# A selective-scan block on one core: nesting over halves of the channels and pairs of states, with b from row-tiled 64-token diagonal blocks

## Chip, cores and metric

The kernel runs on one core of one Trainium2 chip. The metric is the device time of an execution in microseconds (us). One execution of each kernel is also taken by the hardware profiler; its span is given beside the times.

## What is computed

x has 8 rows of 2048 tokens with 512 channels, in fp32. The reference is a layer norm, a selective scan (S6) with a residual, a second layer norm and an int8 matmul with a residual:

```python
xp = jnp.einsum('bld,ed->ble', x, x_proj_w)          # 64 of dt, 16 of B, 16 of C
delta = jax.nn.softplus(jnp.einsum('blr,dr->bld', d_rank, dt_proj_w) + dt_proj_b)
deltaA = jnp.exp(jnp.einsum('bld,dn->bldn', delta, A))
deltaB_u = jnp.einsum('bld,bln,bld->bldn', delta, Bm, x)
    h = dA_t * h + dBu_t
    y = jnp.einsum('bdn,bn->bd', h, C_t)
y = ys.transpose(1, 0, 2) + x * D
...
x = x + _L0_attn_ref(_layernorm(x, axis=-1), ...)
x = x + _L0_ffn_ref(_layernorm(x, axis=-1), ...)     # rows scaled by max|x|/127, rounded, times int8 weights
```

For each of 512 channels and 16 states there is one recurrence over the tokens of a row: h = da * h + b, with da = exp(delta * A) and b = delta * x * B. The output of a channel is the sum of h * C over its states.

## The kernel before

**Tiling.** The tokens are cut into 32 chunks of T = 512, four to a batch row. In a chunk there are 16 states n and 4 tiles d of 128 channels: 64 units of (state, channel tile), and to each unit belongs a *slot* of the order in which instructions are issued. Channels lie on the 128 partitions and tokens along the free axis.

**One unit.** ACT computes da, one exp of 128x512 (exp_unit, L742). PE writes b into one PSUM bank (b_pe, L777 to L796), and DVE runs the scan over 512 tokens (L804), reading da from SBUF and b from PSUM. The b of a unit is made in one of two ways. For the six states of DIAG_STATES, delta * x (tokens on partitions, 128 tokens in each of four blocks) is multiplied by a diagonal matrix with B on its diagonal (L786); these diagonal blocks dg are kept in DRAM, zeroed once, their diagonals are stored for each chunk (store_diagonals, L262) and a state's blocks of 256 KB are loaded in bt_piece (L759). For the other ten states, ACT scales delta * x by B, token by token (bT, L772), and PE transposes it (L795).

**Four units, one state.** POOL starts the group with a carry (L756): it puts the state at the end of the last chunk, times the first da, into the first column. It ends with one product h * c over 128x2048 (c_mult, L830), where c is a row of C loaded from DRAM to all partitions (load_c, L814). ACT keeps the last column (keep_state, L839). PE turns the products back to tokens on partitions and sums them over the states in PSUM (y_pe and y_halves, L860), eleven slots behind the scans, in two row halves of 64. The skip D * x (L881) and the residual x (add_x, L585) are added in the same banks.

**Around the units.** While chunk k is scanned, steps of chunk k+1 (prep) and of chunk k-1 (post) stand in given slots of PREP_AT and POST_AT (LATE_AT for the last two). In prep: norm (L287), transposes (L299), projection (L311), the transposes to BT and their copy (slot 26, L331 and L340), the projection to delta (dt_pe, L350), its softplus on ACT (slots 27, 31, 32 and 34, L360), transposes of delta (dlt_pe, slots 35 to 41, L368) and their product with x (du, L373). In post: the residual copies on ACT (L612), statistics on DVE (L242, L246), nmr on POOL (L252 to L258), the norm z on ACT (slots 29, 29, 32 and 34, L618), the largest absolute value on DVE (amax, slots 33 and 35, L637), scaling, rounding, int8 matmul and output (o_out, L686).

**What sets the order.** Every engine runs its instructions in the order in which the program issues them (pin). In a slot come the state copy and the carry, the product, the load of c, the exps, bT, b two slots ahead, the scan, y and then the planned steps. EXP_NONE names 22 slots without an exp, 28 to 34 among them, and EXP_TWO 22 slots with two:

```python
        want += 0 if slot in EXP_NONE else 2 if slot in EXP_TWO else 1
        while want and slot not in EXP_NONE and ahead < (s + 3) * ND:
            exp_unit(ahead)
```

**Buffers.** da, h and hc have three each (of 4 units), c five, dg two, bT three. PSUM: y in two tiles of two banks, b in three banks, one bank (ps_m) for everything else.

## Time and profile before

| | us |
|---|---|
| median of three runs | 2850.26 |
| lowest and highest | 2842.12, 2853.73 |
| span of the profiled execution | 2848.6 |
| busy in it: POOL | 2771.5 |
| PE | 2739.1 |
| DVE | 2731.4 |
| ACT | 2723.7 |

The profiled execution's own time is not given apart from its span; the median lies 1.7 us above the span. 2048 scans take 2363.2 us of DVE (1201 ns each, starts 1.11 us apart where they follow one another), 511 products 2328.1 us of POOL, 2048 exps 1381.8 us and 1276 pieces of bT 896.5 us of ACT. How to read the views: a busy time overlaps with that of other engines; the waits name the engine whose result came last; a timeline gives start, length, engine, line, operation and count of instructions that follow each other.

### The profile page before, as it was taken

The page shows a single profiled execution, that of the slowest core. Times are in us where ns is not written, and L with a number is a line of the kernel's source. Part 1 is how long each engine was busy: PE and PEld are TensorE (multiplying, and loading weights), DVE is VectorE, ACT ScalarE, POOL GpSimd, SP SyncE. Part 2 cuts the span into 40 slices and gives each one's busy share as a digit, 9 for nine tenths or more (in the row PEclk, how much of TensorE's full clock was granted, in tenths as well). Part 3 has the DMA queues.
Part 4 walks back from the last instruction along what each step waited for, and adds up shares of the span by engine and source line. Part 5 has one row for each costly group of instructions (what it writes and reads, how often), then busy time and mean ns, then how long its engine had stood idle before and what let it go on. Part 6 is the DMA issues. An engine that isn't in the chain of part 4 may idle for free.

```text
span 2848.6 us, 80379 instructions
## 1 busy us (share of the span) xinstructions
PE 2739.1 (96%) x33032; PEld 2357.2 (83%) x33032; DVE 2731.4 (96%) x2949; ACT 2723.7 (96%) x4762; POOL 2771.5 (97%) x1243
## 2 busy tenths in 40 slices
PE   8999999999999999999999999999999999999988
PEld 6888888888888888888888888888888878888877
DVE  6999999999999999999999999999999999999998
ACT  7999999999999999999999999999999999999995
POOL 6899999999999999999999999999999999999998
PEclk9999999999999999999999999999999999999999
DMA  5333343434434334444344343344444443434332
GB/s 151 107 92 95 106 113 109 109 80 105 113 109 116 87 97 110 106 117 105 85 106 111 109 118 85 101 109 106 116 104 89 106 109 109 111 81 102 100 99 71
DMA packets 260528, 295.90 MB, mean 104 GB/s; under 512 B 118144, under 2 KB 118656, under 8 KB 260160
## 3 DMA queue, kind: packets, MB, share of 16 engines
q1 hardware_dynamic: 259104, 290.53, 39.7%
q8 instruction: 259, 4.24, 0.6%
q14 instruction: 109, 0.89, 0.1%
q10 hardware_dynamic: 1056, 0.23, 0.0%
HBM read 252.55 MB, written 38.14 MB: 102 GB/s over the span
## 4 chain that ended last, share of the span: by engine, by line
PE 68%; DMA 9%; DVE 9%; ACT 5%; issue 4%; POOL 3%; SPq 1%; DVEq 0%; POOLq 0%; ACTq 0%
PE pb L786 22%; PE y L860 14%; PE pb L795 13%; DMA dg<-dg 8%; DVE h L804 7%; PE y L585 3%; PE po L677 3%; PE y L881 3%; PE pxp L311 2%; ACT da L742 2%; PE pdl L368 2%; POOL hc L830 2%; PE pz L660 2%; PE pxn L299 2%; ACT bT L772 2%
## 5 line engine op out<-in xcount | busy, mean ns | idle before, releaser
L804 DVE TENSOR_TENSOR_SCAN h<-da,pb 128x512 f32<-128x512 f32 x2048 | 2363.2, 1201 | 91.7 <-PE pb L786 51.7
L830 POOL TENSOR_TENSOR hc<-h,c 128x2048 f32<-128x2048 f32 x511 | 2328.1, 4563 | 20.2 <-DVE h L804 6.8
L742 ACT ACTIVATE da<-delta,a_neg 128x511 f32<-128x511 f32 (+1 forms) x2048 | 1381.8, 716 | 1.0 <-DVE h L804 0.6
L772 ACT ACTIVATE bT<-x,BT 128x512 f32<-128x512 f32 x1276 | 896.5, 715 | 0.0
L786 PE MATMUL pb<-dg,x 128*128 128x128 f32 x6176 | 785.6, 279 | 45.4 <-DMA dg<-dg 39.4
L786 PEld LDWEIGHTS pb<-dg,x 128*128 128x128 f32 x6176 | 739.2, 192 | 86.4 <-DVE h L804 45.5
L795 PE MATMUL pb<-ident,bT 128*128 128x128 f32 x5104 | 720.2, 276 | 23.6 <-DVE h L804 10.9
L795 PEld LDWEIGHTS pb<-ident,bT 128*128 128x128 f32 x5104 | 581.7, 141 | 183.8 <-issue 70.9
L860 PE MATMUL y<-ident,hc 64*128 64x64 f32 x16384 | 613.6, 226 | 1.9 <-DVE hc L899 1.0
L860 PEld LDWEIGHTS y<-ident,hc 64*128 64x128 f32 x16384 | 547.7, 139 | 75.4 <-issue 49.5
L242 DVE BATCH_NORM_STATS2 st<-x 128x6 f32<-128x512 f32 x244 | 156.3, 671 | 0.0
L350 PE MATMUL pdt<-xp,dtproj_sb 128*128 128x512 f32 x248 | 138.5, 640 | 11.9 <-ACT delta L360 11.4
L698 POOL TENSOR_TENSOR z<-z,x 128x1024 f32<-128x1024 f32 x62 | 147.6, 2380 | 0.0
L630 POOL TENSOR_TENSOR x<-x,bias_b 128x1024 f32<-128x1024 f32 x62 | 146.7, 2367 | 0.1
L881 PE MATMUL y<-diag_d,xnT 64*128 64x64 f32 x2048 | 138.7, 275 | 0.0
L881 PEld LDWEIGHTS y<-diag_d,xnT 64*128 64x128 f32 x2048 | 124.8, 188 | 10.7 <-issue 10.7
L677 PE MATMUL po<-wq_sb,qT 128*128 128x512 bf16 x496 | 127.6, 380 | 0.0
L360 ACT ACTIVATE delta<-pdt,dtb_sb 128x512 f32<-128x512 f32 x124 | 84.9, 685 | 44.6 <-PE pdt L350 43.7
L585 PE MATMUL y<-x,ident 128*128 128x256 f32 x512 | 127.4, 381 | 0.0
L311 PE MATMUL pxp<-xnT,xproj_sb 128*96 128x512 f32 x248 | 123.1, 598 | 0.0
L618 ACT ACTIVATE z<-x,nmr,rstd 128x512 f32<-128x512 f32 x124 | 97.1, 807 | 9.5 <-POOL nmr L258 9.5
L585 PEld LDWEIGHTS y<-x,ident 128*128 128x128 f32 x512 | 90.5, 192 | 8.6
(112 smaller groups left out, 1716.9 us busy)
## 6 DMA issues: line engine op xcount, KB each, us to landing
c<-bc SPq DMA_DIRECT2D x512, 256.0 KB, 3.5
dg<-dg SPq DMA_DIRECT2D x191, 256.0 KB, 4.7
x<-in_x_dram SPq DMA_DIRECT2D x64, 512.0 KB, 4.8
x<-in_x_dram SPq DMA_DIRECT2D x31, 1024.0 KB, 6.7
out_dram<-z SPq DMA_DIRECT2D x62, 512.0 KB, 4.6
dg<-zeros SPq DMA_DIRECT2D x12, 256.0 KB, 5.3
dg<-BT SPq DMA_DIRECT2D x192, 2.0 KB, 6.7
x<-in_x_dram SPq DMA_DIRECT2D x4, 256.0 KB, 4.4
```

Of the source, the lines that this page charges most:

```text
L242: pin(nc.vector.bn_stats(st, src))
L311: nc.tensor.matmul(st["pp"][:E], lhsT=xproj_sb[:, d, :], rhs=xn_t[k][:, d, :], start=(d == 0), stop=(d == ND - 1),)
L585: nc.tensor.matmul(ys[k, i // 2][:, half, i % 2, :, :], lhsT=ident, rhs=t[:, :, half, :], start=False, stop=False, skip_group_check=True,)
L677: nc.tensor.matmul(po, lhsT=qt[:, d, :], rhs=wq_sb[:, d, :], start=(d == 0), stop=(d == ND - 1))
L742: nc.scalar.activation(das[s][:, d, own], delta[k][:, d, own], AF.Exp, scale=a_neg[:, d, n : n + 1])
L772: nc.scalar.activation(bts[s][:, i, :], xn[k][:, i, :], AF.Copy, scale=b_t[k][:, i, n : n + 1])
L786: nc.tensor.matmul(pb[:, ts(i, P)], lhsT=xn[k][:, i, ts(d, P)], rhs=bts[s][:, i, :], start=True, stop=True,)
L795: pin(nc.tensor.transpose(pb[:, ts(i, P)], bts[s][:, i, ts(d, P)], ident))
L804: nc.vector.tensor_tensor_scan(hs[s][:, d, :], das[s][:, d, :], pbs.pop(u), 0.0 if k % CPB == 0 else 1.0, ALU.mult, ALU.add,)
L830: pin(nc.gpsimd.tensor_tensor(hc, h, c.unsqueeze(1).to_broadcast([P, ND, T]), ALU.mult))
L860: nc.tensor.matmul(ys[k, i // 2][:, half, i % 2, d, :], lhsT=hc[rows, d, ts(i, P)], rhs=ident[rows, rows], is_transpose=True, start=first, ...
L881: nc.tensor.matmul(ys[k, i // 2][:, half, i % 2, d, :], lhsT=xn_t[k][rows, d, ts(i, P)], rhs=diag_d[rows, d, rows], start=False, stop=Fals ...
```

## The change

The units of a chunk are nested anew: first over the two halves dp of the channels (two tiles each), in each over eight pairs of states, the second half backwards from the last pair. A group is still four units: two tiles by two states, and still has one product on POOL, one carry and one state copy.

The b of both states of a pair is made for one channel tile at once, for all states from diagonal blocks. A block now has 64 tokens: its rows are half of the partitions, its 128 columns are 64 tokens by two states. Eight matmuls, two row halves for each of four blocks, fill a tile of two banks (two such tiles), and the scans read it with a stride of two elements. bT and its ACT instructions are gone. Diagonals are stored by two transfers of 8-byte elements a chunk (six of 4-byte elements before); the blocks of a pair are loaded by 256 KB and its two rows of c by 512 KB, and the last three pairs of the first half are used again at the start of the second. Three blocks are made by POOL at the start; eight zeroing stores go to each DRAM buffer, six before.

So that a block of 64 tokens lies in one bank, tokens are interleaved over the partitions: partition p holds tokens 4p to 4p + 3 in x, and transposes, projections and copies in prep write or read with a stride of four. y has one tile of two banks, used twice a chunk; the residual of the first half is copied in slots 44 and 45, that of the second in 12 and 13 of the next chunk. ps_m has two banks. The add_x matmuls are one for each half. EXP_NONE and EXP_TWO are gone: one exp is issued in every slot, seven ahead. Steps of prep and post keep their slots.

The core of the diff (left out: the start's transposes and projections in the new order of tokens, the tail's copies, and changes of names and shapes alone):

```diff
-DIAG_STATES = [1, 3, 5, 9, 10, 13]
...
-LAST_LOAD = (30, 56)
-LAST_ADD_X = (50, 52, 61, 62)
-SKIP_AT = (43, 46, 55, 60)
-EXP_NONE = (2, 4, 6, 8, 9, 11, 14, 16, 20, 28, 29, 30, 31, 32, 33, 34, 46, 48, 49, 50, 54, 56)
-EXP_TWO = (0, 1, 3, 5, 7, 17, 18, 22, 23, 25, 35, 38, 41, 47, 51, 53, 55, 57, 59, 61, 62, 63)
+MADE_HERE = 3
+REUSED = 3
+LOAD_AT = (18, 20)
+SKIP_AT = (16, 18, 20, 22)
+ADD_X_AT = (24, 26)
+FIRST_HALF_AT = (44, 45)
...
+    dgp = ctx.enter_context(tc.tile_pool(name="dgp", bufs=5))
...
-    ps_b = ctx.enter_context(tc.tile_pool(name="ps_b", bufs=3, space=bass.MemoryType.PSUM))
-    ps_m = ctx.enter_context(tc.tile_pool(name="ps_m", bufs=1, space=bass.MemoryType.PSUM))
+    ps_b = ctx.enter_context(tc.tile_pool(name="ps_b", bufs=2, space=bass.MemoryType.PSUM))
+    ps_m = ctx.enter_context(tc.tile_pool(name="ps_m", bufs=2, space=bass.MemoryType.PSUM))
...
-        pin(nc.sync.dma_start(out=t, in_=xf[k]))
+        pin(nc.sync.dma_start(out=t, in_=xq[k]))
         xn[k] = t
+
+    def turned_tokens(t, i):
+        return t.rearrange("p (q i) -> p i q", i=NT)[:, i]
...
+    dg_dram = [diagd.tile([P, NPAIR, NT, HALF, 2], F32, name=f"dg_{j}") for j in range(2)]
...
     def store_diagonals(k):
         dg = dg_dram[k % 2]
-        for j, n in enumerate(DIAG):
+        row = NPAIR * NT * HALF * 2
+        for h in range(2):
             pin(
                 nc.sync.dma_start(
                     out=bass.AP(
                         tensor=dg.tensor,
-                        offset=dg.offset + j * P * NT * P,
-                        ap=[[NT * P + 1, P], [P, NT]],
+                        offset=dg.offset + h * HALF * row,
+                        ap=[[row + 2, HALF], [HALF * 2, NPAIR * NT], [1, 2]],
                     ),
-                    in_=b_t[k][:, :, n],
+                    in_=b_t[k][ds(h * HALF, HALF)].rearrange("p g i n -> p (g i) n"),
...
+    def turn_tokens(out, src, i, n):
+        pin(
+            nc.tensor.matmul(
+                out,
+                lhsT=turned_tokens(src, i),
+                rhs=ident[:n, :n],
+                is_transpose=True,
+                start=True,
+                stop=True,
+            )
+        )
...
-                pin(nc.tensor.transpose(pt[:, ts(i, P)], xn[k][:, i, ts(d, P)], ident))
+                pin(nc.tensor.transpose(turned_tokens(pt, i), xn[k][:, i, ts(d, P)], ident))
...
-                pin(nc.tensor.transpose(pt[:, ts(d, P)], delta[k][:, d, ts(i, P)], ident))
+                turn_tokens(pt[:, ts(d, P)], delta[k][:, d, :], i, P)
...
+        for s in range(MADE_HERE):
+            dgs[0, s] = dgp.tile([P, NT, HALF, 2], F32, tag="dg", name=f"dg_0_{s}")
+            pin(
+                nc.gpsimd.tensor_tensor(
+                    dgs[0, s],
+                    mask.unsqueeze(1).unsqueeze(3).to_broadcast([P, NT, HALF, 2]),
+                    bt[:, s].unsqueeze(2).to_broadcast([P, NT, HALF, 2]),
+                    ALU.mult,
+                )
+            )
...
+    def add_x(k, dp, half):
+
+        t = x1[k].rearrange("p i (d h c) -> p i d h c", h=2, c=HALF)[:, :, ds(2 * dp, 2), half, :]
+        pin(
+            nc.tensor.matmul(
+                ys[k, dp][:, half, :, :, :],
+                lhsT=ident,
+                rhs=t,
+                start=False,
+                stop=False,
+                skip_group_check=True,
+            )
+        )
...
+    def load_x1(k, j):
+        if j == 0:
+            x1[k] = work.tile([P, NT, DM], F32, tag="x1", bufs=2, name=f"x1_{k}")
+        two = ds(2 * j, 2)
+        pin(nc.sync.dma_start(out=x1[k][:, two, :], in_=xf[k][:, two, :]))
+
+    def residual(k, dp, half):
+        t = x1[k].rearrange("p i (d h c) -> p i d h c", h=2, c=HALF)[:, :, ds(2 * dp, 2), half, :]
+        pin(nc.scalar.copy(t, ys[k, dp][:, half, :, :, :]))
...
+    def place(s):
+        k, g = divmod(s, GROUPS)
+        dp, at = divmod(g, NPAIR)
+        return k, dp, at if dp % 2 == 0 else NPAIR - 1 - at
...
+    def of_unit(u):
+        s, j = divmod(u, 4)
+        k, dp, np_ = place(s)
+        return s, k, 2 * dp + j // 2, 2 * np_ + j % 2, j % 2, j // 2
...
-                das[s][:, d, own], delta[k][:, d, own], AF.Exp, scale=a_neg[:, d, n : n + 1]
+                das[s][:, n2, d2, own], delta[k][:, d, own], AF.Exp, scale=a_neg[:, d, n : n + 1]
...
+    def reused(s):
+        return (s % GROUPS) // NPAIR % 2 == 1 and s % NPAIR < REUSED
...
+        t = dgp.tile([P, NT, HALF, 2], F32, tag="dg", name=f"dg_{s}")
+        pin(nc.sync.dma_start(out=t, in_=dg_dram[k % 2][:, np_]))
+        dgs[k, np_] = t
+
+    def b_pe(v):
...
+        pb = ps_b.tile([P, 2, HALF, NT, 2], F32, tag="b", name=f"pb_{s}_{d2}")
         for i in range(NT):
-            if is_diag(k, n):
+            for h in range(2):
+                rows = ds(h * HALF, HALF)
                 pin(
                     nc.tensor.matmul(
-                        pb[:, ts(i, P)],
-                        lhsT=xn[k][:, i, ts(d, P)],
-                        rhs=bts[s][:, i, :],
+                        pb[:, h, :, i, :],
+                        lhsT=xn[k][rows, i, ts(d, P)],
+                        rhs=dgs[k, np_][rows, i, :, :],
...
+                hs[s][:, n2, d2, :],
+                das[s][:, n2, d2, :],
+                pbs[u // 2].rearrange("p h q i n -> p (h q i) n")[:, :, n2],
...
+        if s >= LAST or reused(s):
             return
-        k, n = divmod(s, N)
-        t = bcp.tile([P, T], F32, tag="c", name=f"c_{k}_{n}")
-        pin(nc.sync.dma_start(out=t, in_=bcs[k][n, :].partition_broadcast(P)))
-        cts[s] = t
+        k, dp, np_ = place(s)
+        t = bcp.tile([P, 2, T], F32, tag="c", name=f"c_{s}")
+        pin(nc.sync.dma_start(out=t, in_=bcs[k][ds(2 * np_, 2), :].partition_broadcast(P)))
+        cts[k, np_] = t
...
+        hc = work.tile([P, 2, 2, T], F32, tag="hc", bufs=3, name=f"hc_{s}")
+        c = cts[k, np_]
+        pin(
+            nc.gpsimd.tensor_tensor(
+                hc, h, c.unsqueeze(2).to_broadcast([P, 2, 2, T]), ALU.mult
+            )
+        )
...
+                    ys[k, dp][:, half, i, d2, :],
+                    lhsT=hc[rows, ts(i, P)],
...
-        plan(k * SLOTS, [(SKIP_AT[i], lambda k=k, i=i: skip_pe(k, i)) for i in range(NT)])
+        plan(k * SLOTS, [(LOAD_AT[j], lambda k=k, j=j: load_x1(k, j)) for j in range(2)])
+        for dp in range(DP):
+            at = (k * DP + dp) * SLOTS // DP
+            plan(
+                at,
+                [(SKIP_AT[i], lambda k=k, dp=dp, i=i: skip_pe(k, dp, i)) for i in range(NT)]
+                + [(ADD_X_AT[h], lambda k=k, dp=dp, h=h: add_x(k, dp, h)) for h in range(2)],
+            )
+        plan(
+            k * SLOTS,
+            [(FIRST_HALF_AT[h], lambda k=k, h=h: residual(k, 0, h)) for h in range(2)],
+        )
...
-            load_c(s + 3)
-
-        want += 0 if slot in EXP_NONE else 2 if slot in EXP_TWO else 1
-        while want and slot not in EXP_NONE and ahead < (s + 3) * ND:
+            load_c(s + 2)
+            load_dg(s + 2)
+        if ahead < (s + 3) * 4:
             exp_unit(ahead)
             ahead += 1
-            want -= 1
         if k < NCHUNK:
-            bt_piece(s + 2, d)
-            b_pe(u + 2)
+            if u % 2 == 0:
+                b_pe(u // 2 + 1)
```

## The prediction

> **What bounds the kernel now.** I read the page's busy times first, then a table of stretches, then the waits of the two busiest engines, then timelines of one chunk.

> ```profile
> PE 2739.1 (96%) x33032; PEld 2357.2 (83%) x33032; DVE 2731.4 (96%) x2949; ACT 2723.7 (96%) x4762; POOL 2771.5 (97%) x1243
> ```

> Four engines over 95% say little: a PE matmul counts as busy until its modelled end, and any of the four could lead. The stretch from 208 to 2736 us, 28.9 chunks of 87.35 us, repeats itself (columns: PE, PEld, DVE, ACT, POOL):

> ```profile
> 208.00:2736.00 2528.00, 2454.16 (x29747) 2111.66 (x29745) 2455.69 (x2628) 2462.24 (x4310) 2497.74 (x1099) 1.00 0.41 104
> ```

> Per chunk that is 86.3 us of work for POOL, 84.85 for DVE, 85.1 for ACT. Their waits in that stretch, largest first:

> ```profile
> POOL ve L252 <- DVE mv L246: 9.4, 20, 0.7
> ```

> ```profile
> DVE h L804 <- PE pb L786: 36.0, 80, 2.0
> DVE h L804 <- PE pb L795: 20.7, 62, 0.6
> ```

> POOL waits 17.8 us in all 28.9 chunks, DVE 64.3 (2.2 a chunk). So POOL is the bound and DVE follows 1.5 us a chunk behind; neither has room. POOL's own list (products 4563 ns each, 16 a chunk, carries, two kinds of additions) is left by the change as it is. It can therefore gain at most the 17.8 us; it can lose as much as DVE is held up beyond POOL's lead.

> **Where the change bites: the order on ACT.** Before, no exp stands in slots 28 to 34, where the four softplus stand. The table is switched twice a chunk:

> ```profile
> L742 ACT ACT_TABLE_LOAD x32 | 41.1, 1283 | 0.6
> L360 ACT ACT_TABLE_LOAD x31 | 39.8, 1283 | 0.6
> ```

> One chunk of it (start, length, what):

> ```profile
> 1463.16 0.20 ACT L340 COPY BT<-pbt 128x64 f32<-128x64 f32 x1
> ...
> 1464.62 1.28 ACT L360 ACT_TABLE_LOAD   x1
> ...
> 1466.59 1.52 ACT L618 ACTIVATE z<-x,nmr,rstd 128x512 f32<-128x512 f32 x2
> ...
> 1471.12 0.81 ACT L618 ACTIVATE z<-x,nmr,rstd 128x512 f32<-128x512 f32 x1
> 1472.35 0.69 ACT L360 ACTIVATE delta<-pdt,dtb_sb 128x512 f32<-128x512 f32 x1 [0.42 <-PE pdt L350]
> 1473.05 1.28 ACT L742 ACT_TABLE_LOAD   x1
> 1474.35 1.95 ACT L742 ACTIVATE da<-delta,a_neg 128x512 f32<-128x512 f32 x3
> ```

> Between one softplus and the next stand norms and state copies, which need no load. From the copy of BT to the end of the last z: 8.8 us. In the changed order every slot issues one exp, seven slots ahead of its scan. From slot 26 ACT runs: BT, e34, load, softplus 0, load, e35, e36, z0, z1, state, e37, e38, load, softplus 1, load, e39, z2, load, softplus 2, load, e40, state, e41, z3, load, softplus 3, load, e42. That is eight loads a chunk for two (251 for 65 in the two built programs). Back to back, by the same timeline, starts lie .61 us apart for exp, .60 for softplus, .70 for z, .10 for a state copy. From BT to the end of z3: 8 x .61 + 6 x 1.29 + 3 x .60 + 4 x .70 + .2 + .1 = **17.5 us**.

> DVE needs z3 for the second amax, in slot 35:

> ```profile
> 1470.53 1.20 DVE L637 TENSOR_REDUCE am<-z 128x2 f32<-128x1024 f32 x1
> 1471.64 2.37 DVE L804 TENSOR_TENSOR_SCAN h<-da,pb 128x512 f32<-128x512 f32 x2
> 1473.92 1.19 DVE L637 TENSOR_REDUCE am<-z 128x2 f32<-128x1024 f32 x1
> ...
> 1479.85 3.43 DVE L804 TENSOR_TENSOR_SCAN h<-da,pb 128x512 f32<-128x512 f32 x3
> ```

> From the scan of slot 26 (1461.42 in this timeline) to that amax are ten scans, two aggregates and one amax: 12.5 us. BT begins about 2.8 us after that scan, since on PE b of the next pair (.90), an add_x matmul (.86) and the transposes for BT (.4) come ahead of it. So z3 ends at 2.8 + .2 + 17.5 = 20.5, and DVE, which runs in order, would stand 8 us at its amax; about 1 us of that it spends earlier, at slot 30, waiting for b. I take **7 us a chunk** (bounds: 3, if BT comes earlier and DVE meets other waits ahead of it; 9). All later scans queue behind the amax. Softplus 3 ends at about 22.5, and the first transposes of delta in slot 35 on PE wait for it, ahead of b of unit 38; that is as late as the amax is, not on top of it.

> How much of this POOL covers shows in the same stretch:

> ```profile
> 1466.51 4.53 POOL L830 TENSOR_TENSOR hc<-h,c 128x2048 f32<-128x2048 f32 x1
> 1471.00 2.36 POOL L630 TENSOR_TENSOR x<-x,bias_b 128x1024 f32<-128x1024 f32 x1
> 1473.31 9.07 POOL L830 TENSOR_TENSOR hc<-h,c 128x2048 f32<-128x2048 f32 x2
> ...
> 1483.15 9.08 POOL L830 TENSOR_TENSOR hc<-h,c 128x2048 f32<-128x2048 f32 x2
> ```

> The product of the group of slots 36 to 39 starts at 1483.15; its last scan is the first of the three at 1479.85 and ends near 1481.05. So POOL has 2.1 us in hand there (median of all chunks 2.1 too, and .4 in groups 4 and 5, the least). A stall of 7 leaves it idle for 7 - 2.1 = 4.9. From then on DVE is the late one and the lead starts from zero; by the pattern of leads POOL then waits up to 1.7 more in groups 4 and 5 of the next chunk. POOL's view: 86.3 + 4.9 + 0 to 1.7 = 91.2 to 92.9. DVE's view: 84.85 + 7 + .8 of other waits = 92.65. I take 92.2, so **+4.85 us a chunk**, in 30 chunks: +145. Chunk 0 has softplus but no z: there the stall comes by the delta transposes, about 6.5 less a lead of 2: +4.5.

> **The rest of the change.** *bT leaves ACT*: 1276 x .61 us are gone, ACT falls to some 2070 us. It was no bound except in places, and its first waits went to DVE through b, so this is worth no more than part of DVE's 2.2 a chunk, which I have already let fall to .8. *b on PE*: the nearest rows are

> ```profile
> 1402.68 1.11 PE L881 MATMUL y<-diag_d,xnT 64*128 64x64 f32 x16
> ...
> 1406.81 1.99 PE L786 MATMUL pb<-dg,x 128*128 128x128 f32 x16
> ```

> L786 runs a record each 112 ns; the row-tiled L881 runs two halves side by side, a pair each 112 ns. New b: per two units, 4 blocks of two halves, two passes, so 8 pairs; 256 a chunk x .112 = 28.7 us, against some 39 before (24 units x .90 and 40 x .44). The bound from above is no overlap, .224 a pair, 57 us. Other PE work is about 41 us a chunk by the distances of starts (16 times 1.14 for y, 4.0 for the skip, 19 for projections, other transposes, add_x and the quantised matmul). PE at 70 is covered by DVE's 85. I take .112, since L881 is also fp32 in two halves. [...] *Interleaved tokens* (four-element strides in transposes, projections and copies): same counts, taken 0, bounds 0 to +2 us a chunk on PE and ACT, which have room outside slots 27 to 34. *Transfers*: dg and c were 22 loads of .26 MB a chunk and become 13 of .26 and 13 of .52, so all traffic rises from 9.2 to 13.7 MB a chunk, 157 GB/s where the stretch from 20 to 26 us moved 332. Their five buffers come free in the order of their loads, and a load waits for a group at least five back: 0.

> The start pays on the queue of SP, which is in order. Before, by the timeline of SP and the DMA view, the first dg load was issued at 37.6 us, behind zeros (6 stores) and the diagonal stores. These took some 10 us for 3072 elements of 4 bytes, and DVE then waited 8.4 us for the dg load. Now 4096 elements of 8 bytes, 2 more zero stores ahead and more load behind: +6 us (bounds +2, +10). Three other PE waits of the start go with the bT units: -3. The tail has residual copies half as large: -2 (0 to -4).

> **Sum.** 2848.6 + 145 + 4.5 + 6 - 3 - 2 = 2999 of span; with the 1.7 by which the median 2850.3 lies above the profiled span: **3000 us**. The bounds of the stall, 3 and 9 (starvation about 1.5 and 7), give 2900 and 3065.

> [...] The row has softplus end at 1473.04, the load start at 1473.05 and the next exp at 1474.35: 1.31 for the whole switch. [...]

> **Rivals.** (1) *Faster*: ACT, relieved of bT, arrives at slot 26 early and DVE's stall stays under POOL's lead of about 2 us, that is, z3 ends by 15 instead of 20.5. For it: ACT loses 28 us a chunk of work. Against: the chain behind BT is serial and none of bT stood between the softplus. POOL alone would remain: 2850.3 - 16 (its waits) + 6 - 3 - 4 = 2833. (2) *PE becomes the bound*: the halves don't overlap at 128 columns; decides above (87.35 - 41)/256 = .18 us a pair. At .224, 98 us and some waits: 3170 to 3330. Against: L881. (3) *The strided scan is slower*: on top of the stall each 10 ns adds .64 us a chunk, 20 us in all; +50 ns gives 3100. (4) *Waits only change places*: the waits for b that go pay for the stall: 2840 to 2865. Against: 2.2 us cannot pay 7.

> **Numbers.** Chances: forecast .73, (1) .10, (2) .04, (3) .07, (4) .06. The range runs from 2890 to 3100: outside are (1), (4) and (2), .20 together. A difference under 0.5%, 14 us, can't be told from none. Faster .09 (most of (1)), same .07, slower .84.

> **What would show it.** Right: some 8 table loads a chunk at 1283 ns; DVE idle about 7 us at the second amax, named as waiting for z; POOL idle some 5 us there, chunks of 92 us; scan 1.20 us; pairs of b each 112 ns; ACT busy near 73%. Wrong: a chunk near 87 (the stall is hidden), pairs over .18 us, a scan above 1.25, or DVE's idle time named for dg or c loads.

## The result and the profile after

The changed kernel takes **3213.79 us** (median, 3213.5 to 3216.97) against 2849.86 for the kernel before: 1.1273 times as long, 95% interval 1.1245 to 1.1300. The forecast was 3000 with a range of 2890 to 3100: the direction held, the size did not. The page of the profiled execution (span 3212.1 us), its busy times and its row of the clock granted to PE in 40 slices:

```profile
PE 2678.7 (83%) x37756; PEld 2152.7 (67%) x37880; DVE 2730.5 (85%) x2950; ACT 2243.9 (70%) x3674; POOL 2765.5 (86%) x1238
...
PEclk8999898989989989989889898898998998988999
```

The clock's row in the kernel before:

```profile
PEclk9999999999999999999999999999999999999999
```

POOL and DVE have the same work as before and are idle for more of the time; no engine became the bound. PE's clock, 9 tenths or more in every slice before, falls to 8 in many. The waits of DVE (us in total, times, longest):

```profile
DVE h L825 <- PE pb L810: 219.0, 197, 11.6
DVE am L649 <- ACT z L630: 215.2, 30, 7.2
```

The second line is the forecast's stall, 7.2 us in each of 30 chunks. The first one is as large, and the forecast did not have it. Where the time went, by the starts of the scans:

| us | first scan | first chunk | mean of the next 30 | from the last chunk's start to the end |
|---|---|---|---|---|
| before | 22.2 | 92.6 | 87.26 | 115.9 |
| after | 32.9 | 102.9 | 98.74 | 113.9 |
| longer by | 10.7 | 10.3 | 30 x 11.48 = 344.5 | -2.0 |

DVE's idle time ahead of the scan of each slot, mean of chunks 1 to 30, and its wait for z, are the figures by which all kernels below are compared:

| us a chunk | 18 | 20 | 30 | 38 to 42 | 46 to 50 | 56 to 62 | z | chunk |
|---|---|---|---|---|---|---|---|---|
| after | 1.14 | .59 | 2.42 | .84 | .28 | 1.48 | 7.17 | 98.74 |
| exps_grouped | 1.04 | .50 | 2.36 | 0 | 1.60 | 1.48 | 0 | 91.78 |
| pe_warm | 0 | 0 | 2.27 | 0 | 1.91 | 1.48 | 7.18 | 97.15 |
| skip_spread | .16 | .14 | .68 | .93 | .36 | 0 | 7.17 | 95.43 |
| grouped_warm | 0 | 0 | 2.22 | 0 | .14 | 1.48 | 0 | 88.09 |
| grouped_spread | .12 | 0 | .63 | 0 | 0 | .90 | 0 | 86.45 |

The kernel before has 2.4 a chunk in all (none over .6 in a slot), the changed one 6.89 besides the wait for z. `skip_spread` also waits 1.39 for transposed delta ahead of du.

**The stall at z.** The table loads in the groups of the page, and ACT's timeline in one chunk:

```profile
L763 ACT ACT_TABLE_LOAD x125 | 160.4, 1283 | 2.2
L372 ACT ACT_TABLE_LOAD x124 | 159.1, 1283 | 2.2
```

```profile
1460.17 0.21 ACT L355 COPY BT<-pbt 128x64 f32<-128x64 f32 x1 [1.29 <-PE pbt L285]
1460.28 0.72 ACT L763 ACTIVATE da<-delta,a_neg 128x511 f32<-128x511 f32 x1
1461.03 1.28 ACT L372 ACT_TABLE_LOAD   x1
1462.37 0.69 ACT L372 ACTIVATE delta<-pdt,dtb_sb 128x512 f32<-128x512 f32 x1
1463.08 1.28 ACT L763 ACT_TABLE_LOAD   x1
...
1477.83 0.80 ACT L630 ACTIVATE z<-x,nmr,rstd 128x512 f32<-128x512 f32 x1
```

From BT (1460.17) to the end of z3 (1478.63) are 18.5 us; 17.5 were forecast. A switch takes 1.31 us from the end of one ACTIVATE to the start of the next (median of 250 loads, the longest 1.37) in `after`. DVE on the other side:

```profile
1468.01 1.19 DVE L649 TENSOR_REDUCE am<-z 128x2 f32<-128x1024 f32 x1
1469.12 2.32 DVE L825 TENSOR_TENSOR_SCAN h<-da,pb 128x512 f32<-128x512 f32 x2
1478.67 1.22 DVE L649 TENSOR_REDUCE am<-z 128x2 f32<-128x1024 f32 x1 [7.22 <-ACT z L630]
```

**The waits for b.** Two things show on PE ahead of slots 18 to 30. First, PE stands idle in slots 10 to 14, where it has little but b and each pair of b waits for a bank (timeline of PE, then the granted clock in stretches of 2 us: length, PE busy, clock, DMA share, GB/s):

```profile
1431.81 0.66 PE L319 MATMUL pxn<-ident,x 128*128 128x128 f32 x4
1433.64 1.16 PE L810 MATMUL pb<-dg,x 64*128 64x128 f32 x16 [1.17 <-DVE h L825]
1437.00 2.08 PE L810 MATMUL pb<-dg,x 64*128 64x128 f32 x16 [2.20 <-issue]
1439.01 1.11 PE L319 MATMUL pxn<-ident,x 128*128 128x128 f32 x4
```

```profile
1434.00:1436.00 2.00, 0.80 (x15) 1.00 0.18 67
1436.00:1438.00 2.00, 1.00 (x9) 0.50 0.05 8
1438.00:1440.00 2.00, 2.00 (x15) 0.50 0.68 249
1440.00:1442.00 2.00, 2.00 (x37) 0.50 0.48 189
1442.00:1444.00 2.00, 2.00 (x40) 0.80 0.88 326
```

The same sixteen records of b take 1.16 us and then 2.08. Slots 12 to 15 of one chunk in the kernel before, then in the changed one (same columns):

```profile
1441.20:1447.67 6.47, 6.47 (x89) 1.00 0.45 161
1633.13:1638.91 5.78, 3.58 (x30) 0.57 0.50 145
```

Second, when work piles up in slots 24 to 27, a pair of b stands behind all of it:

```profile
1457.47 1.16 PE L810 MATMUL pb<-dg,x 64*128 64x128 f32 x16
1458.57 1.12 PE L598 MATMUL y<-x,ident 128*128 128x512 f32 x2
1459.53 0.61 PE L285 MATMUL pbt<-ident,xp 96*128 96x96 f32 x4
1460.07 1.21 PE L885 MATMUL y<-ident,hc 64*128 64x64 f32 x32
1461.21 1.13 PE L362 MATMUL pdt<-xp,dtproj_sb 128*128 128x512 f32 x2
1462.27 2.06 PE L810 MATMUL pb<-dg,x 64*128 64x128 f32 x32
```

Between the end of one pair (1458.6) and the start of the next lie 3.7 us at the full clock, while DVE needs 2.2 for two scans. So the theories: **A**, the loads make the wait for z (and PE's idle time behind it); **B**, the waits for b come of the half clock; **C**, they come of steps crowded into few slots, with b made only one pair ahead.

### The profile page after: what moved, and what is told of

It is laid out like the page before. It is cut to its first block, busy times and chain, and to the rows that moved or that the text cites. A ratio compares the mean times of both kernels' runs of the same rounds, so it can differ in the third digit from the quotient of the medians.

```text
span 3212.1 us, 89337 instructions
## 1 busy us (share of the span) xinstructions
PE 2678.7 (83%) x37756; PEld 2152.7 (67%) x37880; DVE 2730.5 (85%) x2950; ACT 2243.9 (70%) x3674; POOL 2765.5 (86%) x1238
## 4 chain that ended last, share of the span: by engine, by line
PE 57%; ACT 18%; DVE 15%; issue 8%; DMA 1%; POOL 1%; SPq 0%; DVEq 0%; ACTq 0%; POOLq 0%
PE pb L810 24%; DVE h L825 13%; PE y L885 13%; ACT da L763 5%; PE y L598 4%; ACT L763 4%; ACT L372 4%; PE pxp L331 4%; PE y L903 3%; ACT z L630 3%; PE pdl L285 2%; ACT delta L372 2%; PE pz L672 2%; PE pxn L319 2%; DVE z L698 1%
## 5 line engine op out<-in xcount | busy, mean ns | idle before, releaser
L825 DVE TENSOR_TENSOR_SCAN h<-da,pb 128x512 f32<-128x512 f32 x2048 | 2356.2, 1201 | 229.7 <-PE pb L810 219.0
L810 PE MATMUL pb<-dg,x 64*128 64x128 f32 x16384 | 1256.2, 297 | 251.3 <-issue 120.4
L810 PEld LDWEIGHTS pb<-dg,x 64*128 64x128 f32 x16384 | 1080.0, 201 | 526.5 <-issue 391.2
L885 PEld LDWEIGHTS y<-ident,hc 64*128 64x128 f32 x16352 | 613.4, 151 | 78.3 <-issue 65.1
L285 PE MATMUL pdl<-ident,delta 128*128 128x128 f32 x512 | 118.5, 352 | 194.6 <-ACT delta L372 193.6
L678 ACT ACTIVATE qT<-pz 128x512 bf16<-128x512 f32 x124 | 74.0, 597 | 264.6 <-PE pz L672 264.6
L649 DVE TENSOR_REDUCE am<-z 128x2 f32<-128x1024 f32 x62 | 74.8, 1207 | 215.2 <-ACT z L630 215.2
L777 POOL TENSOR_TENSOR da<-first_a,state 128x4 f32<-128x4 f32 x384 | 81.6, 212 | 185.1 <-PE pb L810 76.1
L285 PEld LDWEIGHTS pdl<-ident,delta 128*128 128x128 f32 x512 | 79.3, 211 | 218.0 <-ACT delta L372 203.8
L325 ACT COPY xnT<-pxn 128x512 f32<-128x512 f32 x124 | 72.6, 586 | 178.0 <-PE pxn L319 177.9
L763 ACT ACT_TABLE_LOAD x125 | 160.4, 1283 | 2.2
L372 ACT ACT_TABLE_LOAD x124 | 159.1, 1283 | 2.2
L598 PE MATMUL y<-x,ident 128*128 128x512 f32 x256 | 144.1, 645 | 0.0
```

The source lines that it names most:

```text
L285: nc.tensor.matmul(out, lhsT=turned_tokens(src, i), rhs=ident[:n, :n], is_transpose=True, start=True, stop=True,)
L372: nc.scalar.activation(delta[k][:, d, :], st.pop(("pd", d)), AF.Softplus, bias=dtb_sb[:, d : d + 1])
L598: nc.tensor.matmul(ys[k, dp][:, half, :, :, :], lhsT=ident, rhs=t, start=False, stop=False, skip_group_check=True,)
L763: nc.scalar.activation(das[s][:, n2, d2, own], delta[k][:, d, own], AF.Exp, scale=a_neg[:, d, n : n + 1])
L810: nc.tensor.matmul(pb[:, h, :, i, :], lhsT=xn[k][rows, i, ts(d, P)], rhs=dgs[k, np_][rows, i, :, :], start=True, stop=True,)
L825: nc.vector.tensor_tensor_scan(hs[s][:, n2, d2, :], das[s][:, n2, d2, :], pbs[u // 2].rearrange("p h q i n -> p (h q i) n")[:, :, n2], 0.0 ...
```

## The experiments

Behind each time stand its ratio to the kernel before, measured beside it, and the 95% interval of that ratio.

### The loads alone, taken out and put in

`exps_grouped`, the changed kernel with:

```diff
+EXP_NONE = (28, 29, 30, 31, 32, 33, 34)
+EXP_TWO = (17, 18, 22, 23, 35, 38, 41)
...
-        if ahead < (s + 3) * 4:
+        want += 0 if slot in EXP_NONE else 2 if slot in EXP_TWO else 1
+        while want and slot not in EXP_NONE and ahead < (s + 3) * 4:
```

> The changed kernel with no exp in slots 28 to 34 and seven slots with two, so that the four softplus stand together: 2 table loads a chunk for 8, nothing else changed. Theory A (the loads make the 7.2 us wait for z at the second amax, and by PE's idle time there the half clock behind it): the wait for z falls below 1 us a chunk, the waits for b at slots 38 to 42 (.84) go, those at slots 18, 20, 30 and 62 (5.6) stay: a chunk of 91, 2970 to 3000 us. Rival (DVE's idle time only moves to the next late thing): a chunk over 95, over 3100 us.

3005.57 us, 1.0574 (1.0557 to 1.0592). The wait for z is gone, 38 to 42 too, 18 to 30 and 62 stay: theory A, though the time is 5.6 us above its range, since a wait that was not expected comes at slot 50 (1.47). There PE, no longer late, idles in slots 40 to 44 and falls to half clock (.50 granted in slots 44 to 47 of another chunk):

```profile
1382.34 1.16 PE L812 MATMUL pb<-dg,x 64*128 64x128 f32 x16 [0.33 <-PE pdl L287]
1385.27 2.02 PE L812 MATMUL pb<-dg,x 64*128 64x128 f32 x16 [1.77 <-DVE h L827]
```

`before_split`, the kernel before with `EXP_NONE = ()` and `EXP_TWO = ()`:

> The kernel before with one exp in every slot, so that exps stand between the softplus; nothing else changed. 8 table loads a chunk for 2. Theory A: ACT, 85.1 us busy of 87.3 before, gets 6 x 1.28 = 7.7 more and is the bound with 92.8 a chunk, and DVE waits for z at the second amax: 2990 to 3050 us. Rival (the order of exps is no matter, the loss comes of the new b): within 30 us of 2850.

3101.38 us, 1.0912 (1.0892 to 1.0932): a loss of 259 us by the order of the exps alone, more than expected, and by another way than expected:

```profile
DVE h L804 <- PE pb L795: 287.3, 124, 5.1
PEld pdt L350 <- ACT delta L360: 215.8, 63, 4.8
PE pdt L350 <- ACT delta L360: 198.9, 63, 4.7
```

DVE does not wait for z but for b at slots 34 and 35 (5.06 and 3.52 a chunk). With one bank for everything else, the projection to delta waits on PE until the softplus ahead has read that bank, and b stands behind it. ACT is busy for 93.1 of the 95.5 us of a chunk here, so its sum alone, which the expectation took for the bound (92.8), already asks for most of the loss; how much of the rest is due to that one bank was not tried. The loads cost 7.0 us a chunk in the changed kernel, where ACT is busy for 70.2 of 98.7, and 8.2 in this one.

### Clock or crowding

`pe_warm`, the changed kernel with transposes of the identity where PE idles, results unused:

```diff
+            if d == 1:
+                keep_warm(pt[:, :P], 8)             # xnt_pe, slot 11
+            keep_warm(st["warm"][:, :P], 16)        # new step, slot 12
+                if i == 0:
+                    keep_warm(pt[:, ts(3, P)], {2: 10, 3: 36}.get(d, 0))   # dlt_pe, slot 35
```

> The changed kernel with 70 extra transposes of the identity a chunk on PE, where it stands idle: slots 11 to 13, and ahead of the third and fourth transpose of delta in slot 35. Their results are not used. Theory B (PE is granted half its clock after two idle stretches in each chunk, and works off the backlog late): the clock rises from .91 to about 1.0, the wait for z stays at 7, the waits for b at slots 18, 20 and 30 fall from 4.15 to about 1, those at 38 to 42 from .84 to .2: a chunk of 95, some 3100 us. Theory C (the clock does not matter, the steps on PE are crowded into slots 14 to 31 and 56 to 63): 3200 us or more.

3170.75 us, 1.1157 (1.1140 to 1.1174). Between the two: the waits at 18, 20 and 38 to 42 (2.57 together) vanish, so they came of the half clock; the one at 30 stays (2.27), so it did not; and 1.9 come at 48 to 50, as in `exps_grouped`; the granted clock was .68 to .72 in slots 44 to 51 of one chunk. DVE's waits:

```profile
DVE am L662 <- ACT z L643: 215.3, 30, 7.2
DVE h L838 <- PE pb L823: 193.1, 108, 10.5
```

`skip_spread`, the changed kernel with the matmuls of skip and add_x in other slots:

```diff
-SKIP_AT = (16, 18, 20, 22)
-ADD_X_AT = (24, 26)
+SKIP_AT = ((36, 36, 40, 40), (60, 60, 64, 64))
+ADD_X_AT = ((42, 42), (72, 74))
```

(slots counted from the chunk's start; the last half chunk keeps the old ones)

> The changed kernel with the skip and add_x matmuls in other slots: first half in 36 to 42 for 16 to 26, second half in 60 to 74 for 48 to 58. The exps stay as they are. Theory C (crowding): the waits for b at slots 18, 20, 30 and 62 (5.6 together) fall below 1.5, a chunk of 94 to 95, 3070 to 3100 us. Theory B (clock): only the wait at 62 goes and those at 18 to 30 stay above 3, some 3170 us, unless the matmuls now in slots 8 and 10 keep the clock up by themselves, which the granted clock at these slots would show.

3113.51 us, 1.0956 (1.0939 to 1.0972). 30 falls from 2.42 to .68 and 62 to 0, as theory C has it. 18 and 20 fall too, but not by crowding alone. Between slots 10 and 20 the clock is at half speed for 6.8 us in 27 of the 30 chunks of the changed kernel and for 3.4 in three; here for 3.4 us in 20 chunks and not at all in ten. PE is idle for 2.0 us a chunk in slots 8 to 15 instead of 3.6: the matmuls now in slots 8 and 10 keep the clock up in part, the exception that the expectation names. In chunks with 3.4 us the wait at 18 is about .2 in this kernel, and in five of the seven such chunks of `after` and `exps_grouped`, so it follows the clock; the wait at 20 is .2 here for .55 there, so it needs both causes. The wait for z is as it was; the time is 13.5 us above the expected range, with the 1.39 a chunk for transposed delta that were not expected.

`grouped_warm`: `exps_grouped` with the extra transposes of slots 11 and 12, and four times eight in slots 42 to 45.

> As exps_grouped, with 24 extra transposes a chunk at slots 11 to 13 and 32 at slots 42 to 45 on PE, where it stood idle before its clock fell; skip and add_x where the change put them. Splits the waits for b that are left (7.2 a chunk) into clock and crowding: those at 18, 20 and 48 to 50 (3.1) go if they come of the half clock, those at 30 and 62 (3.8) stay if they come of crowded steps at full clock: a chunk of 88.5 to 89, 2900 to 2920 us. If the clock is no matter: 3000 us.

2892.36 us, 1.0153 (1.0132 to 1.0174). With the clock up in all slices but the first and the last, what is left is crowding alone:

```profile
PEclk8999999999999999999999999999999999999998
```

2.22 at slot 30 and 1.48 at 62, as expected; the time is 7.6 us below the expected range.

### Both edits, and the start

`grouped_spread`: the edits of `exps_grouped` and `skip_spread` together.

> Both edits together: exps kept out of slots 28 to 34, and skip and add_x in the other slots. If the terms add: the wait for z 0, the waits for b 1 to 2 a chunk (.16 + .14 + .68 and up to 1 at 46 to 50), so DVE needs 85.2 + 1.5 = 86.7 and POOL's 86.3 rules: a chunk of 86.5 to 87.5, with the start 11 us later and the first chunk 4 to 8 longer than before: 2855 to 2885 us. Rival (the clock falls in other slots once the loads are gone, as it did at slot 44 with the exps grouped): 89 a chunk, 2920 us.

2840.47 us, .9971 (.9961 to .9980): below the expected range, and **.3% below the kernel before** (10 executions against 13). A chunk is at the lower edge of what was expected, and the first chunk is 1.5 us longer than before, not 4 to 8. The page and the loads:

```profile
PE 2588.7 (91%) x37880; PEld 2062.6 (73%) x37880; DVE 2714.4 (96%) x2950; ACT 1981.9 (70%) x3488; POOL 2762.0 (97%) x1238
```

```profile
L767 ACT ACT_TABLE_LOAD x32 | 41.1, 1283 | 0.6
L376 ACT ACT_TABLE_LOAD x31 | 39.8, 1283 | 0.5
```

POOL is the bound again (idle .6 us a chunk), at 86.45 a chunk for 87.26 before. So the whole 11.48 us a chunk goes when the same steps on ACT and PE are put in another order: the nest, the row-tiled b and the interleaved tokens cost nothing in a steady chunk that such an order doesn't take away. Which of them brings the .8 was not tried.

What is left is the start, 10.7 us to the first scan and a wait of 11.9 for the first dg load. `grouped_spread_zeros`:

```diff
+        zero_diagonals(0)
+        zero_diagonals(1)
         pw = misc("pwarm")
...
-        zero_diagonals(0)
         store_diagonals(0)
...
-        zero_diagonals(1)
```

> As grouped_spread, with the 16 zeroing stores issued at the start, ahead of everything that waits on SP, instead of between the first loads of c and the first dg load. Theory of the start (the dg load of group 3 queues behind them): the wait of 10.5 us at slot 12 of the first chunk goes, less what POOL was behind anyway: 6 to 11 us less than grouped_spread. Rival (other loads are slowed by as much at the start): no gain.

2829.43 us, .9932 (.9912 to .9953). First chunk 83.0 for 94.1: the queue of SP was the cause. `before_zeros`, the same edit in the kernel before:

> The kernel before, with only its 12 zeroing stores issued at the start, ahead of everything that waits on SP. Shows how much of the gain of the regrouped kernels the kernel before could have had: the wait of 8.4 us at slot 12 of its first chunk goes, 2838 to 2843 us; if POOL's work after it does not come earlier, no change, 2847 or more.

2838.85 us, .9966 (.9952 to .9980): about 10 us, so a like gain was open to the kernel before in the time as a whole. Its trace shows only part of it where the edit works: the wait at slot 12 of the first chunk falls from 8.4 to 4.5 us, it does not go, and the first chunk from 92.6 to 88.7. Where the rest comes from stays open. `grouped_spread_zeros_warm` adds transposes at the start:

```diff
         turn(1)
+        for _ in range(14):
+            pin(nc.tensor.transpose(pw[:, :P], ident, ident))
```

> As grouped_spread_zeros, with 14 extra transposes of the identity on PE behind the second block's transposes at the start, where PE stands 1.7 us before its clock falls to half for 12 us; the results are not used. If the half clock delays the first scan (33.6 us against 22.2): first scan 6 to 9 us earlier, 2840 to 2865 us. If the copies with a stride of four on ACT (1.05 us for .58) set the start: 0 to 2 us.

2827.99 us, .9928 (.9903 to .9952), first scan at 32.8 for 33.3. **My theory of the clock fails here.** The 12 us at half clock in the expectation were a misreading: in `after` and `grouped_spread_zeros` the clock is at half for 3.4 us there (12.6 to 16.0 and 11.1 to 14.5). With the extra transposes it was granted in full, and the projections took as long as at half clock. PE is busy without a gap from 12 to 22 us, so no copy on ACT holds them up there (timeline of PE, then the stretch, in this kernel):

```profile
14.35 1.99 PE L489 MATMUL pxp<-xnT,xproj_sb 128*96 128x128 f32 x8
```

```profile
14.00:16.00 2.00, 2.00 (x13) 1.00 1.06 397
```

In the kernel before, eight such records without the stride:

```profile
9.96 1.04 PE L470 MATMUL pxp<-xnT,xproj_sb 128*96 128x128 f32 x8
```

`start_in_order` lets them read in the order in which the transposes wrote:

```diff
-                    xnt.rearrange("p d (q i) -> p i d q", i=NT)[:, i],
+                    xnt_0[:, :, ts(i, P)],
...
-                        rhs=turned_tokens(xnt[:, d, :], i),
+                        rhs=xnt_0[:, d, ts(i, P)],
...
-                        rhs=turned_tokens(xp, i),
+                        rhs=xp_0[:, ts(i, P)],
```

> As grouped_spread_zeros, but at the start of the first chunk the projections read their moving operand in the order in which it was transposed, without the stride of four (the natural order is made later, by four ACT copies in slots 4 to 7 and a second DVE copy). Theory of the start (eight such matmuls take 1.99 us with the stride at the full clock, 1.04 in the kernel before, and the copies on ACT 1.05 for .58): first scan at 24 to 26 us instead of 33.3, total 2820 to 2823 us. Rival (something else sets the first scan): above 31 us, 2828 or more.

First scan at 26.8, and the projections as fast as before once the clock is up:

```profile
16.73 1.04 PE L502 MATMUL pxp<-xnT_start,xproj_sb 128*96 128x128 f32 x8
```

But 2828.55 us in all, .9924 (.9910 to .9939), no less than without: the first chunk takes 86.4, since the diagonals now wait behind the 16 zeroing stores. `start_and_zeros` moves the last eight of them to slots 12 to 19 (the zeros in a tile of their own):

> As start_in_order, with only the first DRAM buffer zeroed at the start and the second one in slots 12 to 19 of the first chunk, since the 16 stores (15 us of issue on SP) were what the first scan's gain ran into: C and the diagonals of the first chunk waited behind them, and DVE 4.8 us for the dg load. If so, first scan at 26 to 27 us, first chunk 82 to 84 instead of 86.4, 2822 to 2826 us. If the dg load is late for another reason: 2828 us.

2823.91 us, .9931 (.9914 to .9948), first scan 27.0, first chunk 82.8 for 86.4. Its time is the lowest of all, .7% below the kernel before; the intervals of it and of `before_zeros` just do not touch (.9948 and .9952). Against `start_in_order` the gain shows in the first chunk and in the times, not in the ratio: the kernel before, measured beside each, took 2843.27 us here and 2849.26 there, so the ratios of the last four versions (.9924 to .9932) can't be told apart.

## Why the prediction was wrong

- **The stall at z**: 7 forecast, 7.17 measured, in the place, by the engine and by the terms that were given. `exps_grouped` shows that the loads are its cause. This step held; that the size came out so closely is in part luck. In the chunk shown BT began 3.8 us after the scan of slot 26 (forecast 2.8) and the chain behind it took 18.5 (17.5), but DVE had spent 2.4 us at slot 30 (1), which took the excess off again.
- **"DVE's view: 84.85 + 7 + .8 of other waits"**: this is the step that failed. The other waits were 6.89. With them DVE's own sum is right: 84.7 busy + 7.17 + 6.89 = 98.7. The 6.1 us between, in 30 chunks, are 183 of the 214 us that were missing. The .8 rested on "PE at 70 is covered by DVE's 85", a sum over a chunk. What decides is the list of PE between two pairs of b: two tiles of b allow one pair ahead, DVE gives 2.2 us for two scans, and slots 24 to 27 alone hold 3.7. The experiments split it: of the waits after, 3.75 (30 and 62 with the clock up) are crowding alone, and 2.57 (18, 20, 38 to 42) go when the clock is kept up; the .6 that remain were not split.
- **PE's lighter list as a gain**: b did get cheaper, the pairs of halves start 112 ns apart as forecast, and L810 has 1256 us busy for the 1506 of the two lines before. But time set free stands in slots 8 to 15 (PE idle for 3.6 us a chunk there, .7 before), and behind it the clock is at half for 6.5 us in slots 12 to 19. Another 8.8 us at half in slots 32 to 39 follow the wait for z, and slots 40 to 47 lower it when that wait is gone (`exps_grouped`) or PE is kept at work in it (`pe_warm`). The forecast counted idle time of PE as free of cost.
- **POOL's lead** of 2.1 and .4: it was not there to be used. POOL idles 12.7 a chunk, 98.74 less its 86: 7.0 ahead of the product of slots 36 to 39, where 4.9 were forecast, and 4.5 ahead of those of slots 12 to 31, where up to 1.7 were, since the waits for b had already made DVE the late one.
- **The most that can be gained**, 17.8 us: this left out POOL's short idle times. The stretch shown in the prediction has 2528.00 - 2497.74 = 30.3 us without work on POOL, and `grouped_spread` gains .8 a chunk, 24 us in 30.
- **The start**: +6 for the dg load, first scan unchanged. The dg load was 3 us later against its scan (wait 11.6 for 8.4), but the first scan itself came 10.7 late. "Taken 0" for the four-element strides is wrong: at the start eight matmul records that read their moving operand so take 1.99 us for 1.04, and the ACT copies 1.05 us for .58. Without both (`start_in_order`) the first scan comes 6.5 earlier; the other 4.6 to the 22.2 of before stay open. The stall of the first chunk came by the delta transposes, 4.6 us of DVE's time where 6.5 were forecast.
- **Scan with stride two, transfers, tail**: 1201 ns before and after; no wait for a steady dg load and one of 1.1 us for c; -2.0 as forecast. The forecast adds nothing for the scan's stride of two, though no row of the kernel before shows a scan that reads so: that was right by luck.
- **ACT's sum**: "some 2070 us" are 69% of 3000 and do not agree with "near 73%"; 2243.9 us were measured, 70% of the longer span.
- **Rivals**: (2) and (3) are out by the 112 ns and the 1201 ns, (4) by waits that grew from 2.4 to 14.1 a chunk. (1) is out too: the stall did not stay under POOL's lead. `grouped_spread` comes near its time, 2840 for 2833, with the loads gone by another order.

Left open: the .9 us that remain at slots 56 and 58 of `grouped_spread`. That one bank more would have spared `before_split` its wait is argued from the waits, and was not tried.

## What to carry to other kernels

When a change drops a hand-written order of issue, count first what that order kept together: here one activation table, worth 7 to 8 us a chunk in either kernel. Weigh an engine that feeds another through few buffers by its list between two of them (here 3.7 us of PE's work against DVE's 2.2), not by its sum per chunk. Work taken from PE leaves idle time there, and idle time has a price when the clock falls with it (here 2.57 us a chunk of DVE's waits): look for what can be moved into it.

## What the runs showed of the hardware

A moving operand read with a stride of four fp32 elements took 1.99 us for eight matmul records of 128 columns at the full clock (`grouped_spread_zeros_warm`, L489), 1.04 without the stride (`start_in_order`, L502). The same stride on the writing side cost nothing where PE wrote PSUM: four transposes took .65 us at L319, .66 at L368 of the kernel before, which writes without a stride. Neither did pieces of 8 bytes: a pair of b at L810 took 112 ns, as did a record of 128 columns at L786 of the kernel before, which writes them in one piece.
